# A two-layer state-space image block: joining the projections and the scans of layer 1 in one list-scheduled stage

## The chip, the cores and the metric

The kernel runs on one core of one Trainium2 chip. The core has five instruction streams that run side by side and meet only through semaphores: PE (matrix multiply), ACT (activations and copies), DVE (elementwise work and scans), POOL (elementwise work) and SP, which here issues all DMA transfers. The metric is device time in microseconds for one execution, the lower the better. Everything is float32.

## The reference, cut to what matters

The input is 4 images of 128x128 positions with 192 channels. Layer 0 is a first state-space block and isn't touched. Layer 1 normalises, projects, runs a 3x3 depthwise convolution and SiLU, and then does four selective scans over the positions of each image: by rows, by rows backwards, by columns, by columns backwards. With `C` = 192 channels, `N` = 16 states and `dr` = 12:

```python
proj = jnp.einsum('kbcl,kcd->kbld', xs, x_proj_w)
dpart, Bm, Cm = proj[..., :dr], proj[..., dr:dr + N], proj[..., dr + N:]
delta = jnp.einsum('kblr,krc->kblc', dpart, dt_w) + dt_b[:, None, None, :]
delta = jax.nn.softplus(delta + dt_b[:, None, None, :])
...
def step(state, inp):
    d, b, c, uu = inp
    dA = jnp.exp(d[..., None] * A_neg[:, None, :, :])
    state = dA * state + (d * uu)[..., None] * b[:, :, None, :]
    y = jnp.einsum('kbcn,kbn->kbc', state, c)
    return (state, y)
```

The four outputs are added, normalised, gated and projected back.

## The kernel before, in words

An image has L = 16384 positions, cut into 16 chunks of T = 1024. Images go in pairs: two images' 192 channels fill three blocks of 128 rows (block 0: 128 channels of the first image, block 1: the remaining 64 of both, block 2: 128 of the second). So there are 2 pairs x 4 directions x 16 chunks = 128 steps, and each step has six halves of 64 channels. A half holds 64 channels in two groups of 8 states, which makes 128 rows; it has NQ = 8 units, one for each state of a group. In all 768 halves and 6144 units.

Layer 1 before has these stages, one after the other: `in_conv`, `projections`, `scans`, `merge` (adds row and column scans) and `layer1_out`.

`projections` loops over pairs, orientations and chunks. It loads the three blocks u, multiplies them with the projection weights (g_pj, line 187 through the helper `mm`) and copies the result to pj (line 857). It stores the rows of C to DRAM (cs). For B it multiplies pj with columns of the identity, so that B comes out with positions on the rows (g_bT, line 860), and spreads each value on a 32-wide diagonal with a mask (dg, line 870, 4096 elements for an image); these diagonals go to DRAM. For each block it then computes delta by matmul (g_dt) and softplus (line 195) and stores it, multiplies it with u on POOL (du, line 885), transposes du on PE (g_dT, line 891), copies that (dT, line 894) and stores it (duT). The tile framework's own scheduler orders this stage.

`scans` reads all of that back. A fill (line 1009) multiplies a 32-row strip of dT with the diagonals D, which puts the product delta*u*B for 8 states into two PSUM banks g_s; ACT copies them into h (line 1027, two copies of 512). Eight fills make the h of one half: 8 x 1024 elements. A unit is then: dA = exp(d * A) on ACT into PSUM (line 1033), the scan along the chunk on DVE in place in h (line 1040), the product with C on POOL (hc, line 1055), and the sum over states by a matmul with a selection matrix (Y, line 1063). After 8 units a half is finished by an addition on DVE (lines 1073 to 1079) and a store, and the last state of each row is kept for the next chunk (st, line 1050). h has two buffers of 8 slots, so a half's fills run during the units of the half before. The order of the scans is written by hand: in unit g the loop issues the fills that the table `AT` gives, the Y of unit g-2, the exponential of unit g+1, the scan of g and the product of g-1.

Layer 0 is ordered by a planner, the class `Order`. Every operation is registered with its engine, a planned cost, what it reads and writes and a rank offset `early`; `emit` simulates the engines and takes, again and again, the operation that can start first, by rank among those that can start at once. It gives each engine a fixed order. The chip runs that order; nothing is rearranged while it runs.

Of the kernel before, what the change touches and what calls it, by code (L numbers as in the profile page):

```python
# [10 lines left out]
F32 = mybir.dt.float32  # L11
# [8 lines left out]
T = R * W  # L20
# [51 lines left out]

class Order:
# [3 lines left out]
    HOP, LOAD, SWITCH, RATE = 0.12, 2.0, 1.28, 250e3  # L77

    def __init__(self):
        self.ops, self.writer, self.readers, self.turn, self.made = [], {}, {}, {}, {}  # L80

    def op(self, engine, cost, fn, reads=(), writes=(), table=None, size=0, early=0):
# [12 lines left out]
        for x in (*reads, *writes):  # L95
# [7 lines left out]
    def emit(self):  # L103
# [13 lines left out]
        for n in range(len(ops)):  # L117
            if not left[n]:
                ready[ops[n][0]].append(n)
        while len(order) < len(ops):  # L120
            best = None
            for e, rs in ready.items():
                for n in rs:
                    at = max(free[e], ready_at[n])
                    ok = True
                    for b in ops[n][4]:
                        if b not in begun:
                            if turn.get(b.queue, 0) != self.turn[b]:
                                ok = False
                                break  # L130
                            ring = rings.setdefault(b.tag, [])
                            if len(ring) >= b.bufs:
                                old = ring[-b.bufs]
# [7 lines left out]
                    if t and t != table:  # L141
                        rank += 20
                    key = (at if at > free[e] + 0.3 else free[e], rank, n)
# [9 lines left out]
            if size:  # L153
                dma = max(dma, end) + size / self.RATE
                done = dma + self.LOAD
# [9 lines left out]
            order.append(n)  # L165
            for m in after[n]:
# [4 lines left out]
                if not left[m]:  # L171
                    ready[ops[m][0]].append(m)
        for n in order:
            ops[n][2]()
# [3 lines left out]
class Maker:  # L178
# [642 lines left out]
    def projections(self, xc, delta, duT, cs, dg, xpw, dtw, dtb2, ident):  # L821
# [3 lines left out]

        nc, tc = self.nc, self.tc
        with tc.tile_pool(name="q_1", bufs=1) as p1, tc.tile_pool(
            name="q_2", bufs=2  # L830
        ) as p2, tc.tile_pool(name="q_ps", bufs=1, space=PSUM) as ps1, tc.tile_pool(
            name="q_ps2", bufs=2, space=PSUM
        ) as ps:
            mask = p1.tile([128, 32], F32, name="mask")
            nc.vector.tensor_tensor(mask, ident[:, 0:32], ident[:, 32:64], ALU.add)
            for q in (2, 3):
                nc.vector.tensor_tensor(mask, mask, ident[:, 32 * q : 32 * q + 32], ALU.add)
            pick = p1.tile([128, 2, NS], F32, name="pick")
            for e in range(2):
                nc.vector.tensor_copy(  # L840
                    pick[:, e], ident[:, 64 * e + DR : 64 * e + DR + NS]
                )
            for p in range(PAIRS):
                for o in range(2):
                    for j in range(NCH):
                        cols = slice(j * T, (j + 1) * T)
                        us = []
                        for i in range(3):
                            u = p2.tile([128, T], F32, tag=f"u{i}", name=f"u{i}")
                            nc.sync.dma_start(u, xc[o][p][i][:, cols])  # L850
                            us.append(u)
                        for kk in range(2):
                            k = 2 * o + kk
                            g = ps1.tile([128, 2, 512], F32, tag="pj", name="g_pj")
                            self.mm(g, [(xpw[:, k, i], us[i]) for i in range(3)])
                            pj = p2.tile([128, T], F32, tag="pj", name="pj")
# [602 lines left out]
```

## Time and profile before

| | |
|---|---|
| time, median of 3 | 28175.08 us (28164.88 to 28178.7) |
| span of the profiled execution | 28177.1 us |
| PE, busy | 23868.8 us (85%) |
| DVE, busy | 22122.1 us (79%) |
| ACT, busy | 20287.8 us (72%) |
| POOL, busy | 19694.8 us (70%) |
| bytes moved by DMA | 5639.07 MB |

These are averages over the whole program. Layer 0 with the transposition ahead of it takes about the first 6500 us, the convolution runs to about 7460, the projections to 10695, the scans to 25890, the merge to 26372 and the output to the end. What a change inside layer 1 is worth has to be read in the windows of those stages. In the lines of groups, the columns are: line, engine, operation, output and inputs by name, shapes, count, then busy us and mean ns of one, then the idle time ahead of them and what ended most of it.

### The profile page before, as it was taken

The numbers are of one execution on the slowest core, as the hardware profiler recorded it, in microseconds if no ns is written. First come the engines' busy times: TensorE is split into PE (matmuls) and PEld (weight loads), VectorE is DVE, ScalarE is ACT, GpSimd is POOL, SyncE is SP. The second block draws the span as 40 slices with busy tenths as digits, with TensorE's granted clock in tenths as the row PEclk, the third lists the DMA queues.
The fourth block names the chain that finished last, engine by engine and source line by source line (L and its number), as shares of the span: only waits on it lengthen the run. The fifth ranks groups of instructions, "written<-read, shape, count | busy, mean of one in ns | idle before, by whom it ended". The sixth has DMA issues, their size and how long they took to land.

```text
span 28177.1 us, 436392 instructions
## 1 busy us (share of the span) xinstructions
PE 23868.8 (85%) x167928; PEld 9146.6 (32%) x167928; DVE 22122.1 (79%) x14982; ACT 20287.8 (72%) x27382; POOL 19694.8 (70%) x9258
## 2 busy tenths in 40 slices
PE   5999999984577778888888888888888888886599
PEld 3333333322233333222222222222222222222355
DVE  4888888889633337999999999999999999998322
ACT  5989898953333337888888888888888888886355
POOL 4777777720122227999999999999999999997000
PEclk7999999997788888999999999999999999998799
DMA  7999999976688887666666666666666666666522
GB/s 214 242 236 243 236 242 238 242 199 197 240 329 330 324 330 203 174 172 162 169 174 175 173 165 166 173 174 173 169 162 174 173 175 175 161 167 201 190 85 79
DMA packets 1992865, 5639.07 MB, mean 200 GB/s; under 512 B 275201, under 2 KB 422081, under 8 KB 1954945
## 3 DMA queue, kind: packets, MB, share of 16 engines
q1 hardware_dynamic: 1990784, 5611.14, 70.6%
q8 instruction: 1329, 21.77, 0.3%
q14 instruction: 752, 6.15, 0.1%
HBM read 3932.77 MB, written 1677.29 MB: 199 GB/s over the span
## 4 chain that ended last, share of the span: by engine, by line
PE 28%; DVE 24%; POOL 11%; issue 8%; ACT 7%; DMA 4%; SPq 1%; POOLq 0%; DVEq 0%; ACTq 0%
DVE h L1040 20%; POOL hc L1055 10%; PE g_s L1009 8%; PE Y L1063 7%; ACT h L1027 2%; ACT dA L1033 2%; DVE acc L806 2%; PE hf L567 1%; PE g_pj L187 1%; PE g_dt L187 1%; POOL du L885 1%; PE g_mean L187 1%; DMA y<-y 1%; PE g_dT L891 1%; DMA delta<-sp_l 1%
## 5 line engine op out<-in xcount | busy, mean ns | idle before, releaser
L1055 POOL TENSOR_TENSOR hc<-h,C 128x1024 f32<-128x1024 f32 x6144 | 14595.7, 2439 | 609.9 <-DVE h L1040 381.3
L1040 DVE TENSOR_TENSOR_SCAN h<-dA,st,h 128x1024 f32<-128x1024 f32 x5760 | 13137.0, 2333 | 237.7 <-ACT dA L1033 213.2
L1063 PE MATMUL Y<-hc,sel 128*64 128x512 f32 x24576 | 6999.3, 649 | 1278.1 <-POOL hc L1055 1273.8
L1033 ACT ACTIVATE dA<-d,alog 128x1024 f32<-128x1024 f32 x6144 | 7035.6, 1145 | 951.8 <-DVE h L1040 890.5
L1027 ACT COPY h<-g_s 128x512 f32<-128x512 f32 x12288 | 6706.7, 611 | 1388.4 <-PE g_s L1009 1387.0
L1009 PE MATMUL g_s<-D,dT 32*64 32x256 f32 x98304 | 7046.9, 406 | 537.0 <-ACT h L1027 518.1
L1009 PEld LDWEIGHTS g_s<-D,dT 32*64 32x64 f32 x98304 | 3290.1, 137 | 6464.2 <-ACT h L1027 4809.1
L445 POOL TENSOR_TENSOR xs<-xs,pr 128x1024 f32<-128x1024 f32 x1536 | 3637.0, 2371 | 334.6 <-ACT pr L440 250.8
L870 DVE TENSOR_TENSOR dg<-g_bT,mask 128x4096 f32<-128x4096 f32 x256 | 1126.1, 4422 | 2083.3 <-PE g_bT L860 1731.9
L588 DVE SCALAR_TENSOR_TENSOR hf<-hh,vec,hf 128x512 f32<-128x512 f32 x3072 | 2318.4, 755 | 422.0 <-PE hf L567 263.8
L1063 PEld LDWEIGHTS Y<-hc,sel 128*64 128x64 f32 x24576 | 1245.1, 138 | 4204.0 <-POOL hc L1055 3040.1
L885 POOL TENSOR_TENSOR du<-sp_l,u 128x1024 f32<-128x1024 f32 x384 | 900.5, 2352 | 2373.3 <-ACT sp_l L195 1846.9
L567 PE MATMUL hf<-sa,diag 96*32 96x512 f32 x18432 | 2154.5, 601 | 14.4 <-DMA sa<-hpad 12.7
L440 ACT ACTIVATE pr<-xi,vec 128x1024 f32<-128x1024 f32 x1536 | 1714.0, 1143 | 301.2 <-POOL xs L445 295.8
L894 ACT COPY dT<-g_dT 128x512 f32<-128x512 f32 x768 | 449.9, 586 | 1137.6 <-PE g_dT L891 987.3
L187 PE MATMUL g_dt<-pj,dtw 128*128 128x512 f32 x1536 | 906.5, 704 | 239.8 <-ACT sp_l L195 239.8
L773 POOL MEMSET xi<- 128x10 f32 x96 | 25.2, 263 | 1477.3 <-DVE acc L806 1224.6
L782 PE MATMUL g_xi<-x,wx 128*128 128x512 f32 x896 | 545.1, 745 | 590.7 <-DVE x L767 527.0
L567 PEld LDWEIGHTS hf<-sa,diag 96*32 96x32 f32 x18432 | 562.6, 109 | 1481.3 <-issue 1388.1
L527 POOL TENSOR_TENSOR dl<-dl,xs 128x1024 f32<-128x1024 f32 x192 | 454.6, 2368 | 838.9 <-ACT dA L525 752.3
L806 DVE SCALAR_TENSOR_TENSOR acc<-xi,vec,acc 128x1024 f32<-128x1024 f32 x768 | 959.4, 1280 | 23.6 <-ACT xi L797 9.4
L187 PE MATMUL g_pj<-u,xpw 128*128 128x512 f32 x1536 | 814.9, 664 | 179.3 <-DMA u<-xc 178.6
(172 smaller groups left out, 21839.4 us busy)
## 6 DMA issues: line engine op xcount, KB each, us to landing
C<-cs SPq DMA_DIRECT2D x4096, 256.0 KB, 6.0
sa<-hpad SPq DMA_DIRECT2D x2304, 276.0 KB, 7.5
dg<-dg SPq DMA_DIRECT2D x256, 2048.0 KB, 7.8
D<-dg SPq DMA_DIRECT2D x1024, 512.0 KB, 4.6
d<-delta SPq DMA_DIRECT2D x1536, 256.0 KB, 4.2
delta<-sp_l SPq DMA_DIRECT2D x384, 512.0 KB, 8.5
duT<-dT SPq DMA_DIRECT2D x384, 512.0 KB, 7.8
dT<-duT SPq DMA_DIRECT2D x768, 256.0 KB, 4.7
```

Source lines behind the costliest of these rows:

```text
L187: nc.tensor.matmul(out[:, h], lhsT, rhs[:, h * 512 : (h + 1) * 512], start=(i == 0), stop=(i == len(terms) - 1),)
L440: op("ACT", 1.1, lambda pr=pr, t=t: nc.scalar.activation(rows(pr()), x()[:, t // 3 : t // 3 + R, t % 3 : t % 3 + W], AF.Copy, scale=v(k, V ...
L445: op("POOL", 2.38, lambda pr=pr: nc.gpsimd.tensor_tensor(o(), o(), pr(), ALU.add), reads=[pr], writes=[o], early=-429)
L567: nc.tensor.matmul(o()[32 * g : 32 * g + 32], diag[:, d, s, k, g], x[:, g, :, c0 : c0 + W], start=(d == 0 and s == 0), stop=(d == 1 and s ...
L588: nc.vector.scalar_tensor_tensor(o3, hh()[:, 1 + dy : 5 + dy, PAD + dx : PAD + dx + W], v(k, V0_K + col), o3, ALU.mult, ALU.add,)
L806: nc.vector.scalar_tensor_tensor(a3, xi[:, t // 3 : t // 3 + R, t % 3 : t % 3 + W], vt[:, V1_CW + t : V1_CW + t + 1], a3, ALU.mult, ALU.add,)
L1009: nc.tensor.matmul(gs[n][64 * jn : 64 * jn + 64, 256 * a : 256 * a + 256], dT[m][rt, 2 * sb + a], D[m // 3, sb][rt, a, 256 * jn : 256 * jn ...
L1027: nc.scalar.copy(dst, src)
L1033: nc.scalar.activation(t, dd[m], AF.Exp, scale=alog[:, c : c + 1])
L1040: nc.vector.tensor_tensor_scan(hq[:, way], dA.pop((m, q))[:, way], hq[:, way], 0.0 if at == 0 else st[hf][:, q : q + 1], ALU.mult, ALU.add,)
L1055: nc.gpsimd.tensor_tensor(t, h[m][:, q], Cq[m // 3, q], ALU.mult)
L1063: nc.tensor.matmul(Yt[m][64 * th : 64 * th + 64], sel, t[:, 512 * th : 512 * th + 512], start=(q == 0), stop=(q == NQ - 1),)
```

## The change: what it does and what it is for

The stages `projections` and `scans` become one, `scans`, and the planner `Order` orders it. While the six halves of a step are scanned, the projections of the next step are done between them: its u is loaded during half 0, the projection starts in half 3, and delta, du and the transposed du follow. The transposed du stays on chip (dT, 4 buffers) and no longer goes through DRAM. The diagonals of B are no longer stored and loaded: for each image and each 256 positions, two small matmuls and one DVE operation of 1024 elements build a tile D directly. delta and C still go through DRAM, since they are read back in another layout or spread over rows.

Further parts:

- h is one tile of 18 slots used as a ring, instead of two buffers of 8. Where a half's slots wrap around, copies into it are split in two.
- The eviction of a fill is one copy of 1024 elements from a PSUM tile of two banks (f), of which there is one. Before, there were three single banks and two copies.
- All projection matmuls and transposes share one PSUM bank (s).
- The order of halves goes through both images of a pair in a step (before: one image after the other), so a projection serves both images. u is loaded for each direction, not once for two.
- Softplus is done in pieces of 512, and the planner is told of the change of activation table. One of three transposed blocks is copied by DVE instead of ACT.
- `Order` gets a window, a penalty `keep` against a change of table, an `idle` threshold, a DMA rate, and `claims` (buffers which an operation must find free before it starts although another fills them).
- wz, avg and wout of the last stage are loaded after the merge instead of ahead of layer 1.

The diff, cut to its core:

```diff
+            od = Order(window=3000, keep=1047, idle=0.500, rate=265e3)
...
+                for c in range(2):
+                    g = bank("P")
...
+                    op("PE", 2.65, mm, reads=[wt, *uu], writes=[g], claims=[t])
+                    op("ACT", 0.59, lambda g=g, c=c: nc.scalar.copy(
+                        t()[:, 512 * c : 512 * c + 512], g()), reads=[g, t], writes=[(t, c)])
...
+                    op("PE", 0.9, lambda g=g, c=c: nc.tensor.matmul(
+                        g(), wt()[:, 1, i], x()[:, 512 * c : 512 * c + 512], start=True, stop=True,
+                    ), reads=[wt, (x, c), x], writes=[g], claims=[l], early=-123)
+                    op("ACT", 0.6, lambda g=g, c=c: nc.scalar.activation(
+                        l()[:, 512 * c : 512 * c + 512], g(), AF.Softplus,
+                        bias=dtb2[:, i % 2, k : k + 1],
+                    ), reads=[g], writes=[l], table="softplus")
...
+                op("POOL", 2.4, lambda: nc.gpsimd.tensor_tensor(u(), l(), u(), ALU.mult),
+                   reads=[l], writes=[u], early=30)
...
+                    op("PE", 0.95, mm, reads=[u], writes=[g], claims=[t], early=-249)
...
+                    if i < 2:
+                        op("ACT", 0.6, lambda turn=turn: turn(nc.scalar.copy), reads=[g], writes=[t], early=-579)
+                    else:
+                        op("DVE", 0.69, lambda turn=turn: turn(nc.vector.tensor_copy),
+                           reads=[g], writes=[t], early=-180)
...
+            def diagonals(s, e, sb):
+                x, t, g = pj[s], buf("D", 5, 128, 2, 512), bank("D")
...
+                op("PE", 0.4, mm, reads=[(x, sb // 2), x], writes=[g], claims=[t], early=-105)
+                op("DVE", 1.2, spread, reads=[g], writes=[t], early=15)
...
-                    h[m] = p2.tile([128, NQ, T], F32, tag="h", name="h")
-                gs = [psS.tile([128, 512], F32, tag="s", name="g_s") for _ in range(2)]
+                    h[m] = [Slot("h", SLOTS) for _ in range(NQ)]
+                td, tD = dT[s, i], D[s, e, sb]
+                gs = buf("f", 1, 128, 2, 512, pool=psF)
...
+                op("PE", 1.12, mm, reads=[td, tD], writes=[gs], claims=h[m])
...
+                op("ACT", 1.13, evict, reads=[gs], writes=h[m])
...
+                op("ACT", 1.16, lambda: nc.scalar.activation(
+                    a(), d(), AF.Exp, scale=alog[:, c : c + 1]),
+                    reads=[d], writes=[a], table="exp", early=-522)
...
+                op("DVE", 2.34, scan, reads=[a, *([s0] if at else [])], writes=[hq])
+                op("POOL", 2.4, lambda: nc.gpsimd.tensor_tensor(t(), hs, tC(), ALU.mult),
+                   reads=[hq, tC], writes=[t])
...
+                op("PE", 0.95, sum_n, reads=[t], writes=[ym], early=-252)
...
+                if s + 1 < len(steps):
+                    if (x, part) == (0, 0):
+                        load_u(s + 1)
+                    if (x, part) == (3, 0):
+                        project(s + 1)
+                    if (x, part) == (3, 4):
+                        for i in range(3):
+                            step_sizes(s + 1, i)
+                if x == 2 and part % 2 == 0:
+                    diagonals(s, 1, part // 2)
+                if x == 5 and part % 2 == 0 and s + 1 < len(steps):
+                    diagonals(s + 1, 0, part // 2)
...
-        mk.projections(xc, delta, duT, cs, dg, xpw, dtw, dtb2, ident)
-    mk.scans(xc, delta, duT, cs, dg, y, ident, alog, dsum)
+    mk.scans(xc, delta, cs, y, w, ident, alog, dsum, dtb2)
```

The numbers after the engine names are the planner's costs in microseconds. `early` is added to an operation's precedence: negative values put it later.

## The prediction

> **What bounds the kernel now.** I read the slices of the page first: they show that layer 1 has three different parts after its convolution. Then I cut the span at the first and last instructions of those parts (busy time by windows; columns: window, length, busy us of PE, PE weight loads, DVE, ACT, POOL with instruction counts, granted clock, DMA share, GB/s).
>
> ```profile
> 7460.00:10695.00 3235.00, 2329.27 (x8192) 1207.46 (x8192) 1126.71 (x261) 988.96 (x1281) 900.48 (x384) 0.82 0.83 328
> 10695.00:25890.00 15195.00, 13383.80 (x122868) 4534.37 (x122868) 14420.60 (x6912) 12770.67 (x19153) 14591.00 (x6143) 0.95 0.64 170
> ```
>
> The first is the projections, the second the scans. They run one after the other, 18430 us together, 143.98 us for each of the 128 (pair, direction, chunk) steps. In the projections no compute engine but PE passes 35%; the DMA share is 0.83. In the scans POOL (96%) and DVE (95%) are nearly full, PE is at 88% and ACT at 84%. So 3235 us are spent with DVE, ACT and POOL mostly idle, before a stage in which they are the limit.
>
> The groups give the durations I use:
>
> ```profile
> L1055 POOL TENSOR_TENSOR hc<-h,C 128x1024 f32<-128x1024 f32 x6144 | 14595.7, 2439 | 609.9 <-DVE h L1040 381.3
> L1040 DVE TENSOR_TENSOR_SCAN h<-dA,st,h 128x1024 f32<-128x1024 f32 x5760 | 13137.0, 2333 | 237.7 <-ACT dA L1033 213.2
> L1027 ACT COPY h<-g_s 128x512 f32<-128x512 f32 x12288 | 6706.7, 611 | 1388.4 <-PE g_s L1009 1387.0
> ...
> L870 DVE TENSOR_TENSOR dg<-g_bT,mask 128x4096 f32<-128x4096 f32 x256 | 1126.1, 4422 | 2083.3 <-PE g_bT L860 1731.9
> ...
> L885 POOL TENSOR_TENSOR du<-sp_l,u 128x1024 f32<-128x1024 f32 x384 | 900.5, 2352 | 2373.3 <-ACT sp_l L195 1846.9
> ```
>
> Note L870 and L885: over 2000 us of idle time each in front of them, against about 1000 us of work.
>
> Then I asked where the scans lose their 5%. Windows of 20 us show it:
>
> ```profile
> 15020.00:15040.00 20.00, 17.52 (x168) 5.88 (x170) 19.86 (x11) 17.61 (x28) 20.00 (x9) 1.00 0.50 138
> 15040.00:15060.00 20.00, 17.87 (x148) 5.86 (x151) 17.12 (x9) 14.89 (x24) 18.02 (x9) 0.83 1.05 244
> 15060.00:15080.00 20.00, 17.75 (x180) 6.10 (x172) 19.99 (x10) 17.84 (x28) 19.35 (x9) 1.00 0.50 137
> ```
>
> DVE is 99% busy except where PE's clock falls; there it loses 2.9 us. The timeline shows the start of such a stretch:
>
> ```profile
> 15047.25 1.08 PE L1063 MATMUL Y<-hc,sel 128*64 128x512 f32 x4 [0.19 <-POOL hc L1055]
> ...
> 15049.58 1.93 PE L1063 MATMUL Y<-hc,sel 128*64 128x512 f32 x4 [1.26 <-POOL hc L1055]
> ...
> 15051.44 1.98 PE L1009 MATMUL g_s<-D,dT 32*64 32x256 f32 x16
> ```
>
> At the end of a half (8 units) all fills are done, PE idles for want of a free h buffer, and the same four matmuls then take 1.93 us instead of 1.08, for some 7 us. Such windows come about every 65 us: 15195/65 x 2.9 = 680 us, most of DVE's 775 us of idle time.
>
> **What the Trainium skill says.** "TensorE: Matmul & The Clock Gate" (Part 1: the HAM clock gate) says that PE runs at half rate after an idle window of about 3.4 us and at full rate after a busy one. The trace agrees on the factor of two and on stretches of about two such windows. "ScalarE: Activation LUTs" (What ACT_TABLE_LOAD costs) puts a switch of table set at 1283 ns plus a drain, 2.66 us in all. The trace shows the 1283 ns, but in layer 0 the next activation begins 0.01 to 0.02 us later and the one before ends 0.02 us earlier, so I take 1.3 us. "PSUM — Partial Sum Buffer" (Specifications) gives eight banks of 512 fp32. The changed scans use dA 2x2, f 2, s 1, Y 1: all eight. No run here shows that limit, but it is why the fill pair f and the projection bank s are single.
>
> **The change part by part, per step of six halves (48 units).**
>
> DVE. The scans and the finishing adds stay: 14420.6/128 = 112.7 us. The diagonals become 8 operations of 1024 elements. L870 is 1.08 ns an element; the nearest row of that size with a PSUM operand is L530 at 1222 ns. Bounds 4422/4 = 1.11 and 1.23; I take 1.22, so 9.8 us. One block's two transposed copies move from ACT to DVE, 0.68 us each by the row of the 512-wide copy from PSUM: 1.4 us. Sum 123.8 us.
>
> POOL. The products with C and with delta stay, 14591 + 900.5 us: 121.0 us. Nothing is added.
>
> PE. Back to back, the chain of waits shows 1.02 us for a fill and 1.01 for a Y: 48 x 2.03 = 97.4. A 512-column matmul record follows the last by 0.43 us, so the 24 records of g_pj and g_dt are 10.3; six groups of transposes at 0.6 are 3.6; 32 small records of B at 1.86/16 are 3.7. Sum 115 us at full clock, 121 at the 0.95 of the scans.
>
> ACT. 12770.7 + 989.0 = 13759.7 us, or 107.5. Two 512-wide evictions become one of 1024: lower bound 1.01 us (pj copy of 1024), upper bound two of 0.61 = 1.22; back to back the old pair took 0.95. A third of the halves wraps the 18-slot ring and needs two instructions. I put this at nothing net. Softplus in halves adds 0.6, two copies gone to DVE save 1.2. New are table loads, since softplus now lies among the exponentials (before, one load served the whole stage). Transposes of a block must go through the one bank before the next block's softplus, and POOL's product (2.35 us) lies between, so the three blocks fall apart: one switch there and back for each is 6 loads, 7.8 us. Bounds: 2 loads (all six together, 2.6 us) and 12 (15.6 us). Sum about 115 us, from 110 to 123.
>
> DMA. The stores and loads of dg, D, duT and dT vanish (2 x 537 + 2 x 201 = 1476 MB); u is read once for each direction (+101 MB). All remaining loads lie beside 125 us of compute per step, where the DMA share was 0.64. I cost it at nothing.
>
> The ring of 18 slots lets a fill start two units before the old pair of buffers did, and PE has projection matmuls to put into the old gap. I expect the half-rate stretches to become rarer, clock 0.96 or more. The loads of wz, avg and wout after the merge, the planner's altered bookkeeping in layer 0: nothing, each hidden behind or equal to what was there.
>
> New waits: each fill waits for the eviction of the last one, since f is single. Behind the waiting fill on PE stand Y sums, so POOL's hc buffers fill up; behind a late eviction on ACT stand the exponentials, for which DVE waits. And the softplus, diagonals and transposes share one bank in turn.
>
> The sums are then DVE 123.8, POOL 121, PE 115, ACT 115. DVE sets the floor, but all four lie within 7%. How close will the listed order come? Layer 0 is ordered by the same planner:
>
> ```profile
> 300.00:6500.00 6200.00, 5813.65 (x27985) 1997.39 (x27986) 4967.30 (x6310) 5115.30 (x5568) 4175.06 (x2577) 0.96 0.93 230
> ```
>
> Its fullest engine, PE, is 94% busy. The hand order of the scans reaches 95% and 96%. I take 95% for DVE: 123.8/0.95 = 130.3 us, x 128 = 16678, plus 40 us to fill the pipe (first projection about 20 us, first scan 26 us after the stage began, partly paid before). 28175 - 18430 + 16678 + 40 = 26463, say 26460 us.
>
> **Rivals.**
> - The floor is reached. If the half-rate stretches vanish and DVE runs at the 99.3% of an undisturbed window: 124.7 x 128 + 40 = 16002, total 25750. For it: those windows, with PE and ACT at 88%. Against it: ACT and PE would now be at 93%, with table loads.
> - The single fill pair becomes the bound. A fill, its eviction and two hand-overs of 0.04 and 0.1 us are 1.09 + 0.04 + 1.01 + 0.1 = 2.24 us. If each eviction finds ACT halfway through an exponential (0.57), 48 x 2.81 = 134.9; two g_pj groups in the way (1.3 each) make 137.5, total 27385. For it: in the groups PE waits for ACT's evictions thousands of times already, with three banks. Against: the planner puts fills and evictions first.
> - Slower. PE falls to the clock of the projections, 0.82, because the waits on single banks leave gaps: 115/0.82 = 140, at 95% busy 147.7 a step, 18906 us, total 28690. A load for each softplus would push the same way. For it: 0.82 was measured with exactly these matmuls. Against: that stage had PE 72% busy; here it has far more to do.
> - No change needs 143.7 a step, between the last two; no mechanism aims there.
>
> **How the numbers follow.** Main case 0.58, floor 0.13, single pair 0.19, slower 0.08, no change 0.02. The faster cases sum to 0.90; I shift 0.01 to slower for the unpriced coupling: 0.89, 0.02, 0.09. The range runs from the floor's 25750 to the single pair's 27400: it leaves out the slow cases and the outer half of those two.
>
> **What would show it.** Right: one stage from 7460 to about 24180 with DVE near 95%, POOL near 93%, clock at least 0.96; no dg, D<-dg, duT or dT<-duT transfers; about 4264 MB moved; some 770 table loads by softplus and exponentials in it; diagonals at 1.22 us; evictions of 1024 at 1.0 to 1.1 us. Wrong: 1500 or more table loads, a clock under 0.9, evictions much over 1.2 us, or DVE's waits led by ACT's dA because of evictions ahead of it. Those would send the time towards the last two rivals.

## The result, and the profile after

The changed kernel takes 27481.96 us at the median (27370.89 to 27548.33), the kernel before 28176.89 in the same session: a ratio of 0.9749, 95% interval [0.9716, 0.9781]. The forecast was 26460, range 25750 to 27400. The direction is right; the gain is 2.5% and not 6.1%. One remark belongs to this number: in two other sessions the kernel before mostly ran at about 27560 us, with a PE clock of 0.943, instead of 28180 with 0.923; against that level the changed kernel is only 0.5% faster (0.9951 [0.9931, 0.997]), and what makes the two levels is not settled.

The windows of the changed kernel; the last row is the joined stage (columns: the stretch, its length, busy time and count of PE, PE weight loads, DVE, ACT and POOL, then PE's clock, DMA share, GB/s):

```profile
300.00:6500.00 6200.00, 5805.59 (x27992) 1994.62 (x27992) 4968.63 (x6312) 5115.40 (x5569) 4176.06 (x2579) 0.96 0.93 230
...
7460.00:25170.00 17710.00, 16242.00 (x133052) 5993.43 (x133052) 15683.95 (x8181) 14688.18 (x17583) 15194.12 (x6518) 0.94 0.48 128
```

Layer 0 is what it was. In the stage DVE is busy for 88.6%, POOL 86%, ACT 83%. From the first scan to the end of the last it takes 17673 us, 138.1 us per step; forecast were 130.3. The groups that answer to those of before:

```profile
L1114 POOL TENSOR_TENSOR hc<-h,C 128x1024 f32<-128x1024 f32 x6144 | 14338.8, 2363 | 2382.5 <-PE Y L1122 1149.2
L1108 DVE TENSOR_TENSOR_SCAN h<-dA,st,h 128x1024 f32<-128x1024 f32 x5760 | 13132.8, 2333 | 765.5 <-ACT st L1138 281.2
L1086 ACT COPY h<-f 128x1024 f32<-128x1024 f32 (+3 forms) x8192 | 6334.2, 799 | 2215.8 <-PE f L1075 2144.5
L1075 PE MATMUL f<-D,dT 32*64 32x256 f32 x98304 | 7157.2, 408 | 786.1 <-ACT h L1086 640.4
...
L1001 DVE TENSOR_TENSOR D<-s,mask 128x1024 f32<-128x1024 f32 x1024 | 1240.2, 1211 | 849.7 <-PE s L995 849.7
...
L962 POOL TENSOR_TENSOR u<-l,u 128x1024 f32<-128x1024 f32 x384 | 907.4, 2363 | 184.6 <-ACT l L955 161.7
```

Durations are as expected. New is the idle time: 2382.5 us ahead of POOL's products (609.9 before), nearly half of it ended by a Y sum on PE, which gives an hc buffer back, and 849.7 us ahead of the diagonals. The chain of the work that ended last, by engine and by line, over the whole program:

```profile
PE 37%; DVE 19%; ACT 13%; issue 6%; DMA 4%; POOL 2%; SPq 1%; DVEq 0%; POOLq 0%; ACTq 0%
DVE h L1108 13%; PE f L1075 13%; PE Y L1122 10%; ACT h L1086 6%; ACT dA L1102 3%; PE s L929 3%; PE s L952 2%; POOL hc L1114 2%; DVE acc L829 2%; PE hf L590 1%; DMA y<-y 1%; DVE D L1001 1%; PE g_mean L210 1%; DMA C<-cs 1%; PE s L995 1%
```

Before, PE had 28% of this chain, DVE 24%, POOL 11%. It now changes hands more often: between 12000 and 20000 us it has 10260 pieces, before 6059.

Windows of 20 us show that one of the prediction's mechanisms got worse:

```profile
15240.00:15260.00 20.00, 18.18 (x169) 7.23 (x162) 18.72 (x11) 17.35 (x21) 19.31 (x9) 1.00 0.42 119
...
15280.00:15300.00 20.00, 19.85 (x108) 6.18 (x108) 13.31 (x8) 11.67 (x18) 13.43 (x6) 0.50 0.28 86
15300.00:15320.00 20.00, 18.87 (x112) 6.54 (x108) 13.78 (x8) 10.16 (x10) 10.30 (x5) 0.50 0.10 27
15320.00:15340.00 20.00, 20.00 (x103) 6.11 (x96) 9.66 (x5) 9.50 (x14) 13.14 (x6) 0.50 0.19 53
```

PE is at half rate for over 60 us on end while the trace has it 94 to 100% busy. Before, such a stretch mostly lasted some 7 us. The timeline of PE at its end:

```profile
15346.39 1.03 PE L995 MATMUL s<-ident,pj 128*128 128x16 f32 x4
...
15351.18 1.98 PE L1122 MATMUL Y<-hc,sel 128*64 128x512 f32 x4
15353.08 1.98 PE L1075 MATMUL f<-D,dT 32*64 32x256 f32 x16
15355.00 4.13 PE L929 MATMUL s<-u,w 128*128 128x512 f32 x6
15359.06 1.09 PE L1075 MATMUL f<-D,dT 32*64 32x256 f32 x16
```

Fills and Y sums in turn (1.98 us each instead of 1.09 and 1.08) did not bring the clock back here; it came back during six full-array matmuls of 512 columns.

From the instruction and clock records I add up when DVE does nothing, between the first scan and the end of the last:

```
us per step     step    DVE works   idle, PE at full rate   idle, PE at half rate
before         118.5      112.7            2.1                     3.8
after          138.1      122.6           10.0                     5.4
```

(The step of before is that of the scans alone.) The new loss is mostly at full rate: 10.0 us per step, of which 5.7 lie ahead of the diagonals and 2.2 ahead of the first scan of a half.

### The profile page after: what moved, and what is told of

The parts are those of the page before. It is cut to its first block, busy times and chain, and to the rows that moved or that the text cites. A ratio compares the mean times of both kernels' runs of the same rounds, so it can differ in the third digit from the quotient of the medians.

```text
span 27482.1 us, 440640 instructions
## 1 busy us (share of the span) xinstructions
PE 24406.1 (89%) x169976; PEld 9399.1 (34%) x169976; DVE 22279.5 (81%) x16004; ACT 21227.8 (77%) x24544; POOL 19417.1 (71%) x9258
## 4 chain that ended last, share of the span: by engine, by line
PE 37%; DVE 19%; ACT 13%; issue 6%; DMA 4%; POOL 2%; SPq 1%; DVEq 0%; POOLq 0%; ACTq 0%
DVE h L1108 13%; PE f L1075 13%; PE Y L1122 10%; ACT h L1086 6%; ACT dA L1102 3%; PE s L929 3%; PE s L952 2%; POOL hc L1114 2%; DVE acc L829 2%; PE hf L590 1%; DMA y<-y 1%; DVE D L1001 1%; PE g_mean L210 1%; DMA C<-cs 1%; PE s L995 1%
## 5 line engine op out<-in xcount | busy, mean ns | idle before, releaser
L1114 POOL TENSOR_TENSOR hc<-h,C 128x1024 f32<-128x1024 f32 x6144 | 14338.8, 2363 | 2382.5 <-PE Y L1122 1149.2
L1108 DVE TENSOR_TENSOR_SCAN h<-dA,st,h 128x1024 f32<-128x1024 f32 x5760 | 13132.8, 2333 | 765.5 <-ACT st L1138 281.2
L1086 ACT COPY h<-f 128x1024 f32<-128x1024 f32 (+3 forms) x8192 | 6334.2, 799 | 2215.8 <-PE f L1075 2144.5
L1075 PE MATMUL f<-D,dT 32*64 32x256 f32 x98304 | 7157.2, 408 | 786.1 <-ACT h L1086 640.4
L1102 ACT ACTIVATE dA<-d,alog 128x1024 f32<-128x1024 f32 x6144 | 6905.3, 1124 | 312.3 <-DVE h L1108 257.1
L1075 PEld LDWEIGHTS f<-D,dT 32*64 32x64 f32 x98304 | 3276.9, 138 | 6683.6 <-ACT h L1086 4810.8
L1001 DVE TENSOR_TENSOR D<-s,mask 128x1024 f32<-128x1024 f32 x1024 | 1240.2, 1211 | 849.7 <-PE s L995 849.7
L962 POOL TENSOR_TENSOR u<-l,u 128x1024 f32<-128x1024 f32 x384 | 907.4, 2363 | 184.6 <-ACT l L955 161.7
L1108 DVE TENSOR_TENSOR_SCAN h<-dA,h 128x1024 f32<-128x1024 f32 x384 | 856.2, 2274 | 59.5 <-ACT dA L1102 27.6
L952 PE MATMUL s<-pj,w 128*128 128x512 f32 x1536 | 894.2, 665 | 6.9 <-ACT l L955 2.2
L210 PE MATMUL g_mean<-y,avg 128*128 128x512 f32 x896 | 393.5, 596 | 480.3 <-DMA y<-y 480.0
```

The source lines that it names most:

```text
L1001: nc.vector.tensor_tensor(t().rearrange("t a (n s) -> t (a n) s", s=32), g()[:, : 2 * NS].unsqueeze(2).to_broadcast([128, 2 * NS, 32]), ma ...
L1075: nc.tensor.matmul(gs()[64 * jn : 64 * jn + 64, n, 256 * a : 256 * a + 256], td()[rt, r // 64, 2 * sb + a], tD()[rt, a, 256 * jn : 256 * j ...
L1086: nc.scalar.copy(H[:, at : at + nq, 256 * sb : 256 * sb + 256].rearrange("p q (a r s) -> p q a r s", a=2, s=32)[:, :, :, 2 * rp : 2 * rp + 2],
L1102: op("ACT", 1.16, lambda: nc.scalar.activation(a(), d(), AF.Exp, scale=alog[:, c : c + 1]), reads=[d], writes=[a], table="exp", early=-522)
L1108: nc.vector.tensor_tensor_scan(hs[:, way], a()[:, way], hs[:, way], 0.0 if at == 0 else s0()[:, q : q + 1], ALU.mult, ALU.add,)
L1114: op("POOL", 2.4, lambda: nc.gpsimd.tensor_tensor(t(), hs, tC(), ALU.mult), reads=[hq, tC], writes=[t])
```

## The experiments

Two theories stood at the start and a third came later. A: the single fill pair is the loop that sets the time, since a fill and its eviction must hand over to each other. B: DVE waits in order for the B matmuls, and the scans queue up behind. C, later: PE, at the clock it is granted, is the bound. Each diff is against the changed kernel and cut. "The list" is the order that the planner gives; some edits keep it, others make it anew, and I say which.

**Table loads (e_exp).** Softplus becomes an exponential, which leaves out the logarithm and with it all switches; the list is the same.

```diff
-                        l()[:, 512 * c : 512 * c + 512], g(), AF.Softplus,
+                        l()[:, 512 * c : 512 * c + 512], g(), AF.Exp,
```

> Softplus is replaced by the exponential in the emitted instruction only, so delta is not the reference's, the planned order is the same and no table load is left in the joined stage (764 loads of 1.283 us, 985 us of ACT time, are gone). If the table switches stand on the path (they delay the evictions, which the single fill pair passes on to PE, and the exponentials, which DVE waits for), the time falls by 500 to 985 us, to 26500 to 27000. If the single pair or the half-rate stretches of PE are what costs, it falls by less than 250 us.

Measured: 27601.89 us (27562.28 to 27650.58). ACT's work falls from 114.7 to 106.8 us per step and nothing is gained: neither the switches nor ACT's work holds the step.

**No projections (e_noproj).** Projections, step sizes and transposes are made for the first chunk of each direction only and used, with its delta and C, for all of its chunks. The list is made anew.

```diff
...
-                if s + 1 < len(steps):
+                if s + 1 < len(steps) and steps[s + 1][2] == 0:
                     if (x, part) == (0, 0):
```

> Projections, softplus, delta*u and its transposes are done for the first chunk of each direction only and reused for the other 15 (this part of the computation is left out); the diagonals, the fills, the units, the planner, the ring and the single fill pair stay. Per step DVE has about 121 us of work, POOL 114, PE 101, ACT 99. If the single pair and the planner's order cost the bubbles by themselves, a step stays above 133 us (stage above 17000 us, total above 26750). If it is the projections put between them, DVE goes back to 97% or more: about 125 us a step, stage 16000, total about 25750. If half-rate stretches start at the transposes of the last block, they should be gone with those: clock of the stage 0.98 or more.

Measured: 26626.59 us (26418.99 to 26688.16), clock 0.90. Idle of DVE at full rate falls from 8.2% of the full-rate time to 2.8%, ahead of the diagonals to 0.2 us per step; yet PE spends 3615 us at half rate instead of 2135. Two things follow. The single pair and the planner's manner alone leave almost no gaps at full rate, so those come in with the projections; whether by their work or by their place in the list, this run can't tell. And half rate doesn't need the transposes.

**Dense matmuls added (e_warm).** Three full-array matmuls of 512 columns per step after the third block's transposes, into the bank s, only to keep PE's clock up; new list.

```diff
...
+                def mm():
+                    for i in range(3):
+                        nc.tensor.matmul(
+                            g(), wt()[:, 1, i], x()[:, :512], start=(i == 0), stop=(i == 2),
+                        )
+                op("PE", 2.65, mm, reads=[wt, (x, 0), x, dT[s, 2]], writes=[g])
```

> One group of three full-array 512-column matmuls (2.6 us at full clock, result not used) is added to each step, after the transposes of the third block, where the half-rate stretches begin. If only such matmuls bring PE back to full rate, the stretches of 40 to 90 us disappear: clock of the stage from 0.94 to 0.965 or more, and DVE's idle time in windows of reduced clock from 837 us to under 450. The time then falls by some 100 to 500 us (27000 to 27400), what is won less up to 339 us of added PE time. If the stretches end for another reason, the clock stays at 0.94 and the time rises by up to 339 us.

Measured: 27798.28 us (27764.98 to 27823.27), 316 more. The stretches at half rate become shorter but more (160 instead of 92; 2306 us in all). Nothing is gained by dense work in that place.

**Another place for the Y sums (e_y0, e_y450).** `early` of the Y sum from -252 to 0, so that it follows its product at once, and to -450, so that sums come in bursts; new lists.

```diff
...
-                op("PE", 0.95, sum_n, reads=[t], writes=[ym], early=-252)
+                op("PE", 0.95, sum_n, reads=[t], writes=[ym])
```

> The sums over states (Y) lose their late rank (early -252 to 0), so the planner puts them ahead of more fills and projections. If POOL's 1042 us of waiting for Y (hc buffers not freed) is a cause of its own, the time falls by 300 us or more. If it is only where the shortage of PE and ACT time shows, that wait shrinks, the waits for fills grow as much, and the time stays within 150 us of 27480.

> The opposite of e_y0: the sums over states are put later still (early -252 to -450), so that several Y come in a run. In the traces PE's half-rate stretches end at a run of 512-column matmuls (g_pj, or six Y in a row) and last while fills and Y alternate one by one. If that is what the clock follows, more runs of Y raise the clock of the stage above 0.94 and shorten the stretches; POOL's waits for Y grow. If the clock follows something else, it stays near 0.94 or falls, and the time rises by what POOL waits more.

Measured: 31361.47 us (31257.62 to 31716.91) with a clock of 0.81, and 28663.7 (28595.67 to 28926.97) with 0.885. The bursts lowered the clock instead of raising it, as I had thought possible. Half-rate time is 10332 and 4904 us. In e_y0 the loss is not only the clock's: DVE's idle time at full rate grows from 10.0 to 18.6 us per step, and POOL's ahead of its products, at full rate too, from 12.3 to 18.8. So putting every sum early is no cure either; in e_y450 DVE's idle time at full rate stays near the old, at 10.8.

**Two fill pairs (e_sb, e_sb_f2, e_sb_f2s2y2).** PSUM has no room for a second pair, so dA moves to SBUF (e_sb is that alone, as a control, with one buffer instead of two for w and prev to make room); then f, and then also s and Y, get two buffers. New lists.

```diff
...
-                a, t = buf("dA", 2, 128, T, pool=psA), buf("hc", 3, 128, T)
+                a, t = buf("dA", 2, 128, T), buf("hc", 3, 128, T)
...
-                gs = buf("f", 1, 128, 2, 512, pool=psF)
+                gs = buf("f", 2, 128, 2, 512, pool=psF)
```

> Control for the next two: the decays dA lie in SBUF (two buffers) instead of PSUM, which frees four banks that nothing uses yet; w and prev have one buffer instead of two to make room. The fill pair f, the bank s and Y stay single. All theories: within 150 us of 27480, unless the scan is slower with both operands from SBUF (the scan row shows it).

> As e_sb, with two fill pairs instead of one. If the single pair makes the bubbles at full clock (PE waits for the eviction, ACT for the fill, DVE idle 7.8%, 1139 us), DVE's share in windows of full clock rises from 0.92 to 0.95 or more, and the time falls by 400 us or more against e_sb. If it is the sheer PE work of the projections between fills, or the single bank s, the share stays under 0.935.

> As e_sb_f2, with two banks s for projections, transposes and diagonals and two Y banks. If the shared bank s holds up the diagonals (DVE waits 850 us for them) and the softplus, the time falls by another 200 us or more, to about 26600, and DVE's waits for s halve. If not, it stays within 100 us of e_sb_f2.

Measured: 37322.65, 39096.97 and 38956.07 us. The control already falls apart. Its groups:

```profile
L1114 POOL TENSOR_TENSOR hc<-h,C 128x1024 f32<-128x1024 f32 x6144 | 25108.1, 4119 | 1251.3 <-PE Y L1122 656.9
L1108 DVE TENSOR_TENSOR_SCAN h<-dA,st,h 128x1024 f32<-128x1024 f32 x5760 | 21995.9, 3866 | 668.9 <-ACT st L1138 311.6
```

With dA in PSUM the products took 2363 and the scans 2333 ns. The Trainium skill, "SBUF — State Buffer" (Who interferes with whom), says that a DVE instruction with two inputs in SBUF and a GpSimd instruction that reads SBUF contend for one read interface; the trace agrees, as both got slower together. Beside so large a change the two variants tell nothing about the pair.

**The pair handed over by halves (e_split).** A second attempt at A, which needs no more PSUM. The list is the same; each fill goes into two single banks, one after the other, and each bank is evicted by itself, so that PE may refill the first while ACT copies the second.

```diff
-                gs = buf("f", 1, 128, 2, 512, pool=psF)
+                gs = Halves(psF, "f", 1, [128, 512])
...
+                    for n in range(2):
+                        for at, q, nq in runs(m):
+                            nc.scalar.copy(
```

> The listed order is kept; only the fill pair of two banks is handed over in halves: PE writes n=0 into one bank and n=1 into another, ACT copies each bank by itself, so that PE's next half fill may begin while ACT still copies the other half. Theory A (the single fill pair is the loop that sets the step: in the trace of the changed kernel the last of a half's eight evictions ends 0.1 us, at the median, before the half's first scan, and fills, evictions and the gaps between them add up to 137.9 us of a 138.1 us step): the loop gets slack of some 0.5 us per pair, 24 us per step, and the step falls until DVE or the order holds it, to about 130 us (total 26400, from 26200 to 26800), DVE share of the stage 93% or more, although ACT gets 5 to 10 us more work per step. Theory B (the scans wait in DVE's queue behind the diagonals' PSUM products, whose matmuls stand late in PE's queue): no change, 27400 to 27700, or slower by ACT's extra work.

Measured: 27592.08 us (27447.23 to 27649.71) beside 27438.54 (27370.96 to 27487.89) for the changed kernel itself on the same chip (a_again). Its group of fills:

```profile
L1085 PE MATMUL f<-D,dT 32*64 32x256 f32 x98304 | 7972.2, 407 | 129.1 <-ACT h L1097 105.1
```

PE's idle time ahead of fills falls from 786.1 to 129.1 us, but the fills themselves are busy for 815 us more (7972.2 instead of 7157.2). Two lines show why:

```profile
15018.67 1.07 ACT L1097 COPY h<-f 128x512 f32<-128x512 f32 x2 [0.42 <-PE f L1085]
15019.59 1.29 PE L1085 MATMUL f<-D,dT 32*64 32x256 f32 x16
```

The fill begins before the eviction ahead of it has ended (at 15019.74), and then takes 1.29 us instead of 1.11. Of 6143 refills 2598 begin so early, yet from the end of an eviction to the end of the next fill it takes 1.23 us at the median, as in the changed kernel. The wait has moved into the fill, and A is not tested by this run. It is by e_halfF below.

**Diagonals left out (e_nodiag).** Built at the first chunk of each direction only, and those of a pair's first image used for both; new list.

```diff
...
-                td, tD = dT[s, i], D[s, e, sb]
+                td, tD = dT[s, i], D[s - steps[s][2], 0, sb]
```

> Leaves out the diagonals of B except at the first chunk of each direction (and uses those of the first half of the states for both halves); all else as in the changed kernel. DVE's work falls by 9.7 us per step, to 112.9. Theory B (scans wait behind the diagonals): the 5.4 us of idle ahead of them go too, about 124 us per step, total 25600 (25400 to 26000). Theory A (single fill pair): the idle only moves from the diagonals to the scans, which then wait for the last eviction; step 134 to 138 us, total 26900 to 27450, DVE share of the stage about 83%.

Measured: 27066.71 us (27055.82 to 27100.21). DVE's work falls by 8.6 us per step, the step by 3.3 (to 134.8). Its group of scans:

```profile
L1108 DVE TENSOR_TENSOR_SCAN h<-dA,st,h 128x1024 f32<-128x1024 f32 x5760 | 13156.6, 2334 | 2222.2 <-ACT h L1086 715.1
```

The idle time ahead of scans is 2222.2 us instead of 765.5: with the diagonals gone DVE waits at the scans, and in all for 13.1% of the full-rate time. Under this list DVE's own work is not what holds the step, and waiting doesn't need the diagonals. B as the only cause falls; as the list is another, the run doesn't say what clearing this one wait would bring under the old one.

> The changed kernel once more, on the chip of this group, as the yardstick: 27370 to 27600 and a clock of 0.92 to 0.94 if it has one level; a second level some 2% lower, as the kernel before showed on one chip, would show as a clock of 0.95 or more.

> The kernel before once more. On one chip it ran at 27542 to 27569 us (clock 0.943) seven times of nine and at 28180 (0.923) twice. If the two levels differ only in PE's half-rate stretches, a profile at the lower level has fewer of them (about 620 us of DVE time less lost) and the same durations of scans, products and copies.

Measured: a_again, the changed kernel, 27438.54 us (27370.96 to 27487.89), its step 137.8 us with 15.2 us of DVE idle; b_again, the kernel before, 27552.35, 27562.51, 28170.69 and 28195.53 us. Its trace is of the 28170.69 and equal to the first one (1502 us at half rate, then 1520), so the question of the expectation stays open.

**Less work for PE, first try (e_quartY, e_halfY).** In the traces of the joined stage with dA in PSUM, but for that without projections, the fullest engine is PE, 90.0 to 95.5% busy, whatever the others do. So theory C: PE at its clock is the bound. The same list, with the sums of one column half left out for some units (2 and 5 of each half in e_quartY, all but the first in e_halfY).

```diff
...
+                        if th == 0 or q not in (2, 5):
                             nc.tensor.matmul(
```

> Same listed order; the sums over the states leave out one of the two column halves (th = 1) for units 2 and 5 of each half, so 12 of 96 Y matmuls per step. PE's work falls by 12 x 0.57 = 6.8 us per step, nothing else changes. Theory C (PE, at the clock it is granted, is the fullest engine and holds the step at about 92% of its time: 91.8% in the changed kernel, 92.2, 92.3, 95.5, 90.0, 92.6 and 91.3% in six variants whose DVE share runs from 72 to 89%): 119.9 / 0.92 = 130 us per step, total 26450 (26300 to 26800). Theory A or B (the handing over of the fill pair, or the queue behind the diagonals): 27250 or more. If PE's clock falls by as much as the work that was taken away, no change and a clock below 0.90.

> Same listed order; the column half th = 1 is summed for the first unit of each half only, so 42 of 96 Y matmuls per step are left out, 24 us of PE per step. Theory C: PE falls to about 103 us and is out of the way, DVE's 122.6 us set the step at 95 to 98% of its time, 125 to 129 us, total 25800 to 26400. Theories A and B: 27000 or more. Against both: with so little to do PE may sit at half rate (clock below 0.85) and the step then stays above 130.

Measured: 27378.11 (27338.16 to 27414.37) and 27502.43 us (27375.06 to 27582.81). The timeline of e_halfY says why this is no test: with two matmul records a sum takes what it takes with four.

```profile
15004.24 1.08 PE L1123 MATMUL Y<-hc,sel 128*64 128x512 f32 x4 [1.35 <-DVE y L1151]
15005.25 1.09 PE L1075 MATMUL f<-D,dT 32*64 32x256 f32 x16
15006.27 1.07 PE L1123 MATMUL Y<-hc,sel 128*64 128x512 f32 x2
```

The two column halves of a sum run side by side in the array, and leaving one out saved nothing.

**Second try (e_thin2, e_thin7).** Same list; units 2 and 5 (or 1 to 7) of each half sum 64 of every 512 columns only.

```diff
...
+                        cols = 64 if q in (2, 5) else 512
```

> The two column halves of a Y sum were seen to run side by side (1.07 us with two matmul records as with four), so the last two runs took no time from PE. Here the Y sums of units 2 and 5 of each half take the first 64 columns of each 512 only: same order, same waits on hc and on Y, but some 0.9 us of PE less in 12 of a step's 48 sums, 10.8 us per step. Theory C (PE at its granted clock, 126.7 us a step, holds the step at 92% of its time): 115.9 / 0.92 = 126 us, unless DVE (122.6 us) takes over at 95 to 98%, 125 to 129 us; total 25900 to 26400. Theories A or B (waits inside the order): 27100 or more, PE share of the stage falling to 85%.

> The Y sums of units 1 to 7 of each half take 64 columns of each 512: 42 of a step's 48 sums, some 38 us of PE less, PE then near 90 us a step at full clock. Theory C: as in the run before, DVE sets the step, 125 to 129 us, total 25800 to 26400; if PE then sits at half rate throughout, its 90 us become up to 180 and the step is longer than before. Theories A or B: 27000 or more with PE idle 30% of the stage.

Measured: 32967.34 us (32828.95 to 33034.63) and 31815.93 (31809.58 to 31828.9). With less to do the kernel gets 20% and 16% slower than the changed kernel. The stage in windows, e_thin2:

```profile
7460.00:30640.00 23180.00, 21899.62 (x133052) 7936.46 (x133052) 15933.26 (x8181) 14602.86 (x17583) 15221.50 (x6518) 0.62 0.36 98
```

PE's clock in the stage falls from 0.94 to 0.62; PE is 94% busy with less work (in e_thin7 the clock is 0.53 and PE 87% busy). This is a loss of the kind that the prediction's slower rival feared: PE at half rate for most of the stage. It is no test of C at full rate.

**Third try (e_halfF, e_quartF).** Same list; fills leave out half of their columns, every fill in e_halfF and every second one in e_quartF, and the eviction reads the half that is made twice.

```diff
...
-                    for a in range(2):
+                    for a in range(1 if True else 2):
                         for n in range(2):
```

> Every fill leaves out half of its columns (a = 1; the eviction reads the other half twice, so ACT's work and all waits stay): some 0.4 to 0.5 us of PE less in each of 48 fills, about 22 us a step, and this time the small 32-row matmuls go while the dense ones stay, so the clock should not fall: 0.93 or more. Theory C (PE is the bound): PE near 104 us, DVE sets the step, idle of DVE at full rate down from 8% to 3% or less as in the run without projections, 125 to 129 us a step, total 25800 to 26400. Theory A or B (waits inside the order at full rate): the idle at full rate stays near 8%, step 134 or more, total 26900 or more.

> The same for every second fill (rp = 0), about 11 us of PE a step. Theory C: 116 / 0.92 = 126 us a step, or DVE's limit, total 25900 to 26500. Theories A and B: no change at full rate, 26900 or more.

Measured: 27479.8 us (27463.12 to 27490.96) and 27528.04 (27521.05 to 27590.22). The stage of e_halfF:

```profile
7460.00:25170.00 17710.00, 15084.80 (x83944) 4385.21 (x83944) 15717.07 (x8187) 14553.84 (x17593) 15197.06 (x6523) 0.84 0.47 128
```

PE is 1157 us less busy than in the changed kernel, although its clock is 0.84 (fewer matmuls, more half rate, as in the run before). DVE's busy time, and the time, are the same to 0.2%. At full rate PE is now idle for 19.9% of the time (9.2% in the changed kernel), and DVE's share of idle time there doesn't fall but rises, from 8.2% to 11.4%. So C falls too, at full rate.

The same run decides A. A fill takes 0.66 us at the median instead of 1.09, the fills 37.1 us per step instead of 55.9, and the evictions are as long as in the changed kernel. A fill, its eviction and the next fill follow each other within 0.15 us both times in 867 of 6143 cases instead of 2696. The loop of the pair has slack, and the step is 138.0 us as it was. A falls.

**What the kernels with the same list have in common** (from first scan to last, us per step; PE busy is at the clock it had; e_thin2 and e_thin7, which have the list too but were at half rate for most of the stage, are left out; in e_split PE's busy time contains the wait that moved into its fills):

```
            step    DVE idle   PE busy   ACT busy   half rate, us in all
after      138.1      15.4      126.7     114.7       2135
e_exp      138.6      16.2      127.8     106.8       2503
e_split    138.0      15.4      131.8     117.7       2135
e_quartY   137.1      14.5      125.6     114.7       1869
e_halfY    138.7      16.0      127.4     114.7       2443
e_quartF   138.5      15.9      121.5     114.0       3600
e_halfF    138.0      15.2      117.6     113.6       5486
```

ACT was relieved of 7.9 us, PE of 9.1, the pair of 18.8 us of fills. DVE is idle for 14.5 to 16.2 us in each. The idle time goes with the list, not with the load of PE or ACT; DVE and POOL were not relieved under this list.

One such place, in all engines' timeline of the changed kernel; it comes back in each step:

```profile
15889.61 1.08 PE L1122 MATMUL Y<-hc,sel 128*64 128x512 f32 x4 [0.73 <-POOL hc L1114]
...
15890.61 1.09 PE L1075 MATMUL f<-D,dT 32*64 32x256 f32 x16
...
15891.64 2.84 PE L929 MATMUL s<-u,w 128*128 128x512 f32 x6
...
15894.41 1.09 PE L1075 MATMUL f<-D,dT 32*64 32x256 f32 x16
...
15895.43 2.84 PE L929 MATMUL s<-u,w 128*128 128x512 f32 x6
...
15898.20 1.09 PE L1075 MATMUL f<-D,dT 32*64 32x256 f32 x16
...
15899.23 1.13 PE L952 MATMUL s<-pj,w 128*128 128x512 f32 x2
...
15900.28 1.08 PE L1122 MATMUL Y<-hc,sel 128*64 128x512 f32 x4
...
15901.51 4.69 POOL L1114 TENSOR_TENSOR hc<-h,C 128x1024 f32<-128x1024 f32 x2 [4.04 <-PE Y L1122]
...
15902.32 1.94 PE L1122 MATMUL Y<-hc,sel 128*64 128x512 f32 x8
...
15904.18 1.13 PE L952 MATMUL s<-pj,w 128*128 128x512 f32 x2
...
15905.35 0.69 ACT L955 ACTIVATE l<-s,vec 128x512 f32<-128x512 f32 x1 [0.79 <-PE s L952]
...
15906.26 1.08 PE L1122 MATMUL Y<-hc,sel 128*64 128x512 f32 x4
...
15907.27 0.62 PE L995 MATMUL s<-ident,pj 128*128 128x16 f32 x4
...
15907.93 1.22 DVE L1001 TENSOR_TENSOR D<-s,mask 128x1024 f32<-128x1024 f32 x1 [2.86 <-PE s L995]
```

From 15890.61 to 15900.28, for 9.7 us, PE serves the projection of the next step (L929, L952) and three fills, in the order of the list, and no Y sum. So no hc buffer comes free, and POOL, which has three, stands for 4.04 us. From 15900.28 PE makes up for it: four sums, two fills and a step-size matmul, back to back until 15907.27. Only then does the B matmul (L995) come, though the one bank s which it needs has been free since ACT read it, at 15906.04. DVE was done with its scans at 15905.07 and stands for 2.86 us, with the next scan behind the diagonal in its queue; for the first 0.97 us of this the bank was still in use, by a step-size matmul and its softplus; for the next 1.23 PE was at the fill and the sum ahead in its list; the rest is the B matmul itself. Averaged over the steps, POOL's wait in this place (ahead of unit 6 of the third half) is 4.5 us in the changed kernel, 4.4 in e_split and e_exp, 5.3 in e_halfF, and 0.7 without projections. All POOL idle time is 19.3 us per step, against 4.5 before; but without projections it is 19.7, so POOL's idle time as such doesn't tell what DVE loses. The diagonals' wait at the start of the fourth half, 2.8 us per step, is 2.8 in e_split and 2.2 in e_halfF.

## Why the prediction was wrong

- Right: the work. DVE 122.6 us per step (forecast 123.8), POOL 118.8 (121), ACT 114.7 (115). Diagonals take 1.211 us (1.22), evictions of 1024 elements 1.01, each of 764 table loads (770) 1.283 us; 4265 MB are moved (4264). The switches cost no time, as e_exp shows, so my figure for them doesn't matter here.
- Failed: "I take 95% for DVE". It is 88.8% between first and last scan. The forecast left DVE 6.5 us of idle time per step, it had 15.4; less 1.2 us of work that I had too much, that is 7.7 us per step, 986 of the 1022 us by which the time was missed. I had the 95% from a hand order with one job and from layer 0's planner. In e_noproj the same planner with the same buffers does leave DVE only 2.8% of gaps at full rate; with the projections in the list, 8.2%. Of these, neither less work for ACT nor less for PE nor a looser fill pair under the same list took anything noticeable away. I had named the wait, "Behind the waiting fill on PE stand Y sums, so POOL's hc buffers fill up", and gave it no cost. The timeline above shows it, with the projection in the place of the waiting fill. It shows two more that had no cost: the one bank s, which I had named, and the B matmul, for which DVE waits, behind a sum that was put off, which I had not. What each of them adds to the 7.7 us was not measured.
- Failed: "the half-rate stretches to become rarer, clock 0.96 or more". They are rarer (92 instead of 219) but longer: 2135 us instead of 1520, clock 0.94. DVE's idle time that falls into them is 5.4 us per step. Before it was 3.8, or 488 us in all and not the 680 that I had worked out; and in the line that I showed for it PE's wait is for a product of POOL (1.26 us), not for an h buffer. I leaned on the Trainium skill, "TensorE: Matmul & The Clock Gate" (Part 1: the HAM clock gate), where an idle window of about 3.4 us starts the half rate and a busy one ends it. This trace has PE 94 to 100% busy at half rate for 60 us. Nor does it show an idle window at the start: in the 3.4 us ahead of the 92 stretches PE was never idle for more than 1.7 us at once and was busy for 65% of them at the median (before: 55%). The measurement decides.
- PE's work was put at 115 us at full clock, 121 at 0.95; busy are 126.7. This did not set the time, since e_halfF with 117.6 takes the same.
- The rival of the single pair gave 27385, 0.4% from the result, by luck: e_halfF gives the pair slack and gains nothing. Its added term, two g_pj groups in the way of others on PE, is seen in the trace, but it is the Y sums that they put off, not the pair.
- The slower rival did not come true, but e_thin2, one small edit away, is slower still: 32967.34 us.

What stays open. That neither PE's nor ACT's work nor the fill pair sets the idle time is shown by kernels with the list in common; that the order itself does is what is left, and how one wait leads to the next is read from the traces at one place of the step and not tested by itself. e_y0, which moves the sums, is slower also at full rate. e_nodiag warns that DVE can be idle elsewhere when one of the places is cleared under a new list. A fourth hc buffer under the same list, or a list with Y sums between the projection's matmuls, was not run. Nor is it settled why the clock falls and comes back when it does. No run that computes everything beat the changed kernel.

## What to carry to other kernels

When work is put into the gaps of a pipeline whose four engines then stand at 83 to 92%, the sum of the fullest engine alone was no forecast here: ask for each added instruction which buffer's return stands behind it in its queue, and how many buffers the waiting engine has. To find what binds a fixed order, relieve one engine at a time under that same order: if no relief moves the time, suspect the order. Check in the trace that the relief took place, since a wait can move into what counts as busy. Taking matmuls away can slow a kernel down, so look at the granted clock before drawing a conclusion from such a run.

## What the hardware showed that I had not expected

- A PE that the trace has nearly always busy can be at half rate for most of a stage. Shortening 12 of 48 sums per step took the stage's clock from 0.94 to 0.62, at 94% busy, and cost 20%.
- Half rate began without an idle window: the longest idle time of PE in the 3.4 us ahead of any of 92 stretches was 1.7 us.
- The two column halves of a Y sum took 1.08 us together and one of them alone 1.07 us.
- With both operands of the scan in SBUF, beside POOL's products, a scan took 3.87 us instead of 2.33 and a product 4.12 instead of 2.36.
